# A two-layer block (window attention, then a scanned convolution): residuals laid into PSUM banks, row sums on ScalarE, accumulating DMAs, and the seven-product form from group 4 on

## The chip, the cores and the metric

The kernel runs on one core of a Trainium2 chip. The time is the device time of one execution in microseconds, lower is better. Before the change it is 2599.14 us, the median of 3 runs (2598.45 to 2602.19). All data is float32.

A core has a matrix engine (TensorE, PE in the profile; its weight loads are PEld), VectorE (DVE), ScalarE (ACT), GpSimd (POOL), and SyncE (SP), which here only issues DMAs. Each engine runs its own list of instructions in order, and waits for the others through semaphores. PSUM is the small memory that TensorE writes; it has banks, and a bank can be written again once its reader is done.

## The reference, cut to what matters

The input x has 2 images of 56 x 56 tokens with 384 channels. Two layers follow each other.

```
# layer 0
x = x + neighbourhood_attention(layer_norm(x)) @ w_proj + b_proj
x = x + gelu(layer_norm(x) @ w1 + b1) @ w2 + b2           # 384 -> 1536 -> 384
# layer 1
p      = layer_norm(x) @ w_in + b_in                      # 384 -> 768
local  = depthwise 3x3 convolution of p, padded
mixed  = 0.25 * (lr + rl + tb + bt) + local
x = x + layer_norm(mixed) @ w_out + b_out                 # 768 -> 384
x = x + gelu(layer_norm(x) @ w1 + b1) @ w2 + b2           # 384 -> 1536 -> 384
```

Each of `lr`, `rl`, `tb`, `bt` is a running average, y[i] = 0.6 y[i-1] + 0.4 local[i], along the rows forwards and backwards and along the columns forwards and backwards. The last step gives the output.

## The kernel before, in words

The attention takes the first 650 us or so and isn't touched. What follows works on token groups: 49 tiles of 128 tokens, a group being 4 tiles (512 tokens).

**The first pass** (13 groups: group 0 has one tile, groups 1 to 12 have four) computes the MLP of layer 0 and `p`. One step of the loop at L1712 does for its group g: 12 calls of `hidden` (L1191: 3 matmuls of 512 columns into a PSUM bank of which there are three, then a Gelu by ScalarE out of it), then `project_in` (L1471) for the group before, 6 times 3 matmuls with a ScalarE eviction each, stored to `p_d` in DRAM, then `tokens` (L1199) for 4 tiles, 12 matmuls of 384 columns each, in two banks by turns. VectorE takes each of these banks: it adds the residual `x` (L1846) and takes mean and variance of the sum (`Norm.add`, L214). In between, `ahead_of(m)` and `behind(m)` put a 1/12 of the work for the neighbouring groups after each hidden block: normalizing the previous group's result and the next group's input (ScalarE, L245), their statistics (VectorE), their transposes (TensorE) with the copy out of the bank (ScalarE, L262). Groups 1 and 2 compute the MLP by "seven products": a 2 x 2 block product done with seven block multiplications instead of eight (`hidden_by_seven`, L1536, `tokens_by_seven`, L1620), with the sums of blocks on GpSimd and VectorE. Group 3 is half of each form; from group 4 on the form is plain.

**The convolution** runs beside the matmuls from group 3 on, on VectorE. It works on 6 blocks of 128 channels. A `Band` (L1237) is a stretch of image lines of one block: it loads `p` from DRAM, ScalarE makes the centre tap (L1263), VectorE adds the eight other taps (L1281), stores `loc` to DRAM, scans the rows both ways (`both_ways`, L1225), adds `loc` (L1297) and stores the sum to `mix_d`. When all bands of an image are done, six `Columns` (L1306) follow: each loads `loc` of one block in two halves, turns it so that columns lie along the lines (four strided copies per half of the columns, by ScalarE, L1328; the first of a row of Columns by GpSimd), scans both ways in pieces of 14 lines (L1228, L1232), and adds the turned-back result to `mixed`, which was loaded from `mix_d` (L1355), then stores it.

**The second pass** (groups 0 to 12 again, the last of one tile) computes the rest: for each group `measure` (transposes of `mixed` by TensorE and their statistics by VectorE), `project_out` (L1434: `w_out`, 6 matmuls of 384 columns per tile, added to `x` by VectorE at L1440, with statistics), then `hidden`, `tokens` and the store. Up to group 5 the form is plain (loop L1885), from group 6 (`half_way`, the first group that reaches into image 1) it is by seven products (loop L1926). There VectorE also does the transposes, so that the convolution has to be over before: `beside.until` (L1390) puts all that is left of it into the program at that point, and the buffers of the seven-product form take the convolution's place.

**The planner** `Beside` (L115) sets the order. After each piece of the main work the program calls `beside.go(worth)`: it adds `rate * worth` to a budget, and steps of the convolution are written into the program until the budget is used up; each step says what it takes (`us(lines)`, L1221). `worth` is `MLP` = 2.25 per hidden block, `PRO` = 2.5 per block of `project_in`, `ROW` = 6.2 per tile of `tokens`, in the second pass 2.15, 2.5 and 7.0. So the planner decides, when the program is made, between which instructions of the main work each convolution instruction stands on every engine. `beside.later` issues a DMA one step later. Jobs are put on the list in `project_in` when enough groups of `p` exist (`BANDS`, L63): for image 0 after groups 2, 4, 5, 6, for image 1 after groups 8, 10 and 12.

## Time and profile before

| | |
|---|---|
| median of 3 runs | 2599.14 us |
| the profiled execution | 2598.4 us, its span 2596.6 us |
| PE busy | 2570.7 us, 99% |
| DVE busy | 1964.2 us, 76% |
| ACT busy | 982.9 us, 38% |
| POOL busy | 467.0 us, 18% |
| one plain group of the first pass, PE | 79.94 us |
| one plain group of the second pass, PE | 81.28 us |
| one group of the second pass by seven products, PE | 71.86 us |

The page gives busy time by engine, then the span in 40 slices (each digit is the busy share in tenths), then groups of instructions by line. In such a group stand the line, the engine, the operation, what it writes and reads, the count, then the busy time in us and the mean of one in ns, then the idle time ahead of it and what ended it. Instructions of one engine overlap a little, so that from one start to the next is shorter than "the mean of one": for ScalarE about 0.10 us shorter. One matmul in float32 stands as two records.

### The profile page before, as it was taken

The numbers are of one execution on the slowest core, as the hardware profiler recorded it, in microseconds if no ns is written. First come the engines' busy times: TensorE is split into PE (matmuls) and PEld (weight loads), VectorE is DVE, ScalarE is ACT, GpSimd is POOL, SyncE is SP. The second block draws the span as 40 slices with busy tenths as digits, with TensorE's granted clock in tenths as the row PEclk, the third lists the DMA queues.
The fourth block names the chain that finished last, engine by engine and source line by source line (L and its number), as shares of the span: only waits on it lengthen the run. The fifth ranks groups of instructions, "written<-read, shape, count | busy, mean of one in ns | idle before, by whom it ended". The sixth has DMA issues, their size and how long they took to land. (4 is left out here: it accounts for less than half of the span.)

```text
span 2596.6 us, 39994 instructions
## 1 busy us (share of the span) xinstructions
PE 2570.7 (99%) x16146; PEld 1644.1 (63%) x16148; DVE 1964.2 (76%) x3481; ACT 982.9 (38%) x1748; POOL 467.0 (18%) x457
## 2 busy tenths in 40 slices
PE   9999999999999999999999999999999999999999
PEld 5666666666798644555555555555555557888888
DVE  4888878887444288688998889889988836888871
ACT  5656555654443332322344423212233312333222
POOL 0111211121552100000010000000010042344432
PEclk9999999999999999999999999999999999999999
DMA  7423454225311132332346534533354321111000
GB/s 230 154 85 98 155 191 141 86 93 192 114 34 37 59 128 84 109 115 100 127 153 237 199 120 168 180 124 122 105 213 172 136 101 46 49 49 49 22 13 18
DMA packets 131652, 299.17 MB, mean 115 GB/s; under 512 B 10390, under 2 KB 85760, under 8 KB 129152
## 3 DMA queue, kind: packets, MB, share of 16 engines
q1 hardware_dynamic: 126512, 269.76, 30.2%
q10 hardware_dynamic: 4944, 26.74, 3.0%
q8 instruction: 129, 2.11, 0.3%
q14 instruction: 67, 0.55, 0.1%
HBM read 180.86 MB, written 115.61 MB: 114 GB/s over the span
## 5 line engine op out<-in xcount | busy, mean ns | idle before, releaser
L1185 PE MATMUL mm<-hT,w 128*128 128x512 f32 x1080 | 473.6, 593 | 0.1
L1281 DVE SCALAR_TENSOR_TENSOR loc<-pt,taps,loc 128x990 f32<-128x990 f32 (+9 forms) x336 | 377.2, 1123 | 10.2 <-ACT loc L1263 1.9
L1185 PEld LDWEIGHTS mm<-hT,w 128*128 128x128 f32 x1080 | 201.8, 190 | 239.0 <-issue 231.4
L227 POOL TENSOR_TENSOR rs<-rs,mhalf 128x4 f32<-128x4 f32 (+4 forms) x72 | 89.3, 1240 | 1269.9 <-DVE rs L224 1261.3
L1196 ACT ACTIVATE hid<-mm,chan 128x512 f32<-128x512 f32 x180 | 123.3, 686 | 405.9 <-PE mm L1185 405.8
L1203 PE MATMUL y<-w,hid 128*128 128x384 f32 x792 | 260.9, 486 | 0.0
L1203 PE MATMUL y_end<-w,hid 128*128 128x384 f32 x792 | 260.8, 486 | 0.0
L551 DVE TENSOR_TENSOR pts<-sc,bias 119x448 f32<-119x448 f32 (+5 forms) x396 | 219.3, 617 | 45.4 <-PE sc L540 45.1
L561 ACT ACTIVATE pts<-pts 119x448 f32<-119x448 f32 (+5 forms) x396 | 210.9, 573 | 112.1 <-DVE pts L551 107.2
L1203 PEld LDWEIGHTS y_end<-w,hid 128*128 128x128 f32 x792 | 149.9, 190 | 102.8
L1203 PEld LDWEIGHTS y<-w,hid 128*128 128x128 f32 x792 | 149.8, 190 | 102.8 <-issue 0.5
L394 PE MATMUL ps<-hT,wqkv 128*128 128x448 f32 x504 | 204.8, 550 | 2.1 <-ACT vs L439 1.5
L1185 PE MATMUL mm<-hT,w_in 128*128 128x512 f32 x396 | 172.0, 593 | 1.5 <-DVE hid_u L1571 0.9
L394 PEld LDWEIGHTS ps<-hT,wqkv 128*128 128x128 f32 x504 | 91.3, 189 | 84.4 <-issue 74.2
L1185 PEld LDWEIGHTS mm<-hT,w_in 128*128 128x128 f32 x396 | 75.0, 190 | 96.2 <-issue 91.9
L1168 DVE STREAM_TRANSPOSE hT<-xn 32x96 f32<-32x96 f32 x464 | 125.0, 269 | 11.6 <-ACT xn L245 5.6
L245 ACT ACTIVATE xn<-xc,sh,rs 128x384 f32<-128x384 f32 x98 | 64.4, 699 | 170.2 <-DVE sh L238 170.1
L1414 DVE STREAM_TRANSPOSE turned<-mx 32x192 f32<-32x192 f32 x336 | 124.0, 369 | 4.4
L580 PE MATMUL o<-pts,vt 100*32 100x112 f32 (+3 forms) x3168 | 117.0, 265 | 1.8 <-ACT pts L561 1.8
L540 PEld LDWEIGHTS sc<-qT,kT 32*100 32x100 f32 (+3 forms) x3168 | 87.8, 169 | 46.9 <-DVE sum L570 7.6
L540 PE MATMUL sc<-qT,kT 32*100 32x112 f32 (+3 forms) x3168 | 106.5, 268 | 3.5 <-DVE pts L551 3.5
L610 PE MATMUL ps<-wproj,og 128*128 128x384 f32 x294 | 106.4, 501 | 2.8 <-DVE og L523 2.1
(179 smaller groups left out, 4144.4 us busy)
## 6 DMA issues: line engine op xcount, KB each, us to landing
loc<-loc_d SPq DMA_DIRECT2D x24, 784.0 KB
mixed<-mix_d SPq DMA_DIRECT2D x24, 784.0 KB
mix_d<-mixed SPq DMA_DIRECT2D x24, 784.0 KB
xa<-x_d SPq DMA_DIRECT2D x24, 768.0 KB
bias<-in_bias_t ACTq DMA_DIRECT2D x13, 1344.0 KB
p_d<-mx SPq DMA_DIRECT2D x11, 1536.0 KB
mx<-mix_d SPq DMA_DIRECT2D x11, 1536.0 KB
pt<-p_d SPq DMA_DIRECT2D x18, 560.0 KB
```

Of the source, the lines that this page charges most:

```text
L394: nc.tensor.matmul(ps, lhsT=wqkv[:, c, m * P : (m + 1) * P], rhs=hT[:, c, half_of(n)], start=c == 0, stop=c == NC - 1,)
L540: nc.tensor.matmul(sc[i // 2][: w.keys, i % 2, q : q + TT], lhsT=kT[d, hg, w.keys_at + r * w.kc : w.keys_at + (r + w.rows) * w.kc], rhs=qT ...
L551: nc.vector.tensor_tensor(self.pts[:n, h : h + 2, lo:hi, :], sc[half][:n, :, at * TT : (at + hi - lo) * TT].rearrange("p h (c q) -> p h c ...
L561: nc.scalar.activation(t, t, AF.Exp)
L580: nc.tensor.matmul(o[i * HD : (i + 1) * HD, self.slot, :TT], lhsT=w.vt[:n, c, h * HD : (h + 1) * HD], rhs=self.pts[:n, i, c, :], start=c = ...
L610: nc.tensor.matmul(ps, lhsT=ogs[t // 7][:, c, at : at + P], rhs=wproj[:, c, :], start=c == 0, stop=c == NC - 1,)
L1168: nc.vector.transpose(hT[j : j + HD, :, k * P + i : k * P + i + HD], xn[i : i + HD, k, :].rearrange("p (c q) -> p c q", c=NC)[:, :, j : j ...
L1185: nc.tensor.matmul(ps[:, : n * P], lhsT=w[:, c, m * P : (m + 1) * P], rhs=hT[:, c, : n * P], start=c == 0, stop=c == NC - 1,)
L1196: nc.scalar.activation(t[:, : n * P], ps[:, : n * P], AF.Gelu, bias=col(b1, m))
L1203: nc.tensor.matmul(ps, lhsT=t[:, k * P : (k + 1) * P], rhs=w[:, m, :], start=m == 0, stop=m == len(lhs) - 1,)
L1281: nc.vector.scalar_tensor_tensor(to, pt[:, lo + dy - self.top : hi + dy - self.top, xt : xt + n], self.tap(dy, dx), to, ALU.mult, ALU.add,)
L1414: nc.vector.transpose(t[j : j + HD].rearrange("p (m c) -> p m c", m=NI)[:, :, i : i + HD], mx[i : i + HD, :, k * P + j : k * P + j + HD],)
```

## The change

- **Residuals laid into banks.** From group 3 of the first pass on, ScalarE copies the residual tile `x` into the PSUM bank (`seeded`), and the matmuls of `tokens` add onto it. VectorE's addition at L1846 goes.
- **Sums and statistics by ScalarE.** `ByScalar` takes the place of `Norm` for groups 3 and later, for the result and for the next group's input: `take` (ScalarE copy with a sum, and one GpSimd multiplication), `spread` (ScalarE Square with a sum) and `close` (four small GpSimd operations instead of one on VectorE and one on GpSimd).
- **Mixed channels by accumulating DMAs.** A Band stores `loc` into `mix_d` as well, ScalarE scales the scanned rows, and a DMA issued by GpSimd adds them to `mix_d` in DRAM. A Columns no longer loads `mixed`: ScalarE turns the scanned lines back, scaled (`turn_back`), and two DMAs add the halves to `mix_d`. VectorE's L1297 and L1355 go. Scans of Columns are one over 28 lines instead of two over 14.
- **Bias rows by accumulating DMAs.** `add_row` is a DMA issued by GpSimd instead of an addition on VectorE or GpSimd. `b_out` is added after `mix` has been loaded, in the second pass.
- **Seven products from group 4 on** in the second pass instead of from group 6 (`switch = 4`), with `beside.until` after `project_out` of group 4.
- **The planner's numbers:** `MLP`, `OUT`, `ROW` = 2.6, 3.9, 7.8, the rate 0.96 throughout, and in the second pass `STATS` = 0.75 is taken off the budget for each statistic that VectorE still does.

```diff
@@ class Beside
-        self.late, self.rate = [], 0.9
+        self.late, self.rate = [], 0.96
...
-    def later(self, issue):
+    def later(self, issue, steps=1):
-        self.late.append([1, issue])
+        self.late.append([steps, issue])
...
-    def go(self, worth):
-        self.due += self.rate * worth
+    def go(self, worth, own=0.0):
+        self.due += self.rate * worth - own
@@ class ByScalar (new)
+        def take(self, k, ps, out):
+            at = slice(k, k + 1)
+            nc.scalar.activation(out, ps, AF.Copy, accum_out=self.sum[:, at])
+            nc.gpsimd.tensor_tensor(self.off[:, at], self.sum[:, at], per_c[:, at], ALU.mult)
+        def spread(self, k, x, junk):
+            at = slice(k, k + 1)
+            nc.scalar.activation(
+                junk, x, AF.Square, bias=self.off[:, at], accum_out=self.var[:, at]
+            )
+        def close(self, k):
+            rs, tt = self.rs[:, :k], nc.gpsimd.tensor_tensor
+            tt(rs, self.var[:, :k], eps_c[:, :k], ALU.add)
+            tt(rs, rs, mhalf[:, :k], ALU.pow)
+            tt(rs, rs, root[:, :k], ALU.mult)
+            tt(self.sh[:, :k], self.off[:, :k], rs, ALU.mult)
@@ passes
-        half_way = next(g for g, (t, n) in enumerate(dgroups) if t + n * P > T1)
+        switch = 4
@@ def add_row
-            engine = nc.vector if beside.busy() else nc.gpsimd
-            engine.tensor_tensor(
-                x[:, :n, :], x[:, :n, :], row(name).unsqueeze(1).to_broadcast([P, n, C]), ALU.add
+            nc.gpsimd.dma_start(
+                out=x[:, :n, :], in_=row(name).unsqueeze(1).to_broadcast([P, n, C]),
+                accum_op=ALU.add,
             )
@@ new
+        def seeded(x, k):
+            ps = bank()
+            nc.scalar.copy(ps, x[:, k, :])
+            return ps
+        def primed(t):
+            nc.tensor.matmul(t, lhsT=zeros[:, :P], rhs=zeros[:, : t.shape[1]], start=True, stop=True)
@@ Band.steps
-                beside.later(lambda: nc.sync.dma_start(
-                    out=loc_d[self.b][self.m, :, at], in_=flat(loc)))
-                both = half("both", "out", 3)[:, : self.n]
...
-                nc.vector.scalar_tensor_tensor(
-                    flat(both), flat(both), share, flat(loc), ALU.mult, ALU.add
-                )
...
+                for to in (loc_d, mix_d):
+                    beside.later(lambda to=to: nc.sync.dma_start(
+                        out=to[self.b][self.m, :, at], in_=flat(loc)))
+                both = half("both", "out", 4)[:, : self.n]
+                yield from both_ways(both, loc)
+                behind = beside.behind()
                 if isinstance(behind, Band):
                     behind.centre()
+                beside.later(lambda: nc.scalar.mul(flat(both), flat(both), share), 5)
+                beside.later(lambda: add_to_mix(self.b, self.m, at, both), 8)
+        def add_to_mix(b, m, at, src):
+            nc.gpsimd.dma_start(out=mix_d[b][m, :, at], in_=flat(src), accum_op=ALU.add)
@@ Columns.steps
+                def turn_back(c):
+                    if not mixed:
+                        mixed.extend(half("mixed", "out", 4) for h in range(2))
                     for i in range(0, HALF, QUARTER):
                         at = slice(c * HALF + i, c * HALF + i + QUARTER)
                         for h in range(2):
-                            nc.vector.scalar_tensor_tensor(
-                                to, t[:, i : i + QUARTER, h * HALF : (h + 1) * HALF]
-                                .rearrange("p w h -> p h w"), share, to, ALU.mult, ALU.add,
+                            nc.scalar.mul(
+                                mixed[h][:, :, at],
+                                self.lines[c][:, i : i + QUARTER, h * HALF : (h + 1) * HALF]
+                                .rearrange("p w h -> p h w"), share,
                             )
+                for c in range(2):
+                    if c == 1:
+                        behind = beside.behind()
+                    for step, took in enumerate(both_ways(self.lines[c], self.lines[c])):
+                        if c == 0 and step == 0:
+                            self.turn(nc.scalar.copy)
+                        yield took
+                    beside.later(lambda c=c: turn_back(c), 1 + c)
                 if isinstance(behind, Columns):
                     behind.turn(nc.scalar.copy)
                 for h in range(2):
+                    beside.later(lambda h=h, at=at: add_to_mix(self.b, self.m, at, mixed[h]), 3)
@@
-        MLP, PRO, ROW = 2.25, 2.5, 6.2
-        MLP_D, OUT_D, ROW_D = 2.15, 2.5, 7.0
+        MLP, OUT, ROW = 2.6, 3.9, 7.8
+        STATS = 0.75
@@ first pass, groups 4 and later (before: statistics by VectorE at m == 3, normalizing from m == 7)
+                    if g >= EARLY.stop and 2 <= m < 2 + n_next:
+                        norm_next.take(m - 2, x_next[:, m - 2, :], xn_next[:, m - 2, :])
+                    if g >= EARLY.stop and 3 <= m < 3 + n_next:
+                        norm_next.spread(m - 3, x_next[:, m - 3, :], xn_next[:, m - 3, :])
+                    if g >= EARLY.stop and m == 2 + n_next:
+                        norm_next.close(n_next)
+                    if to <= m < to + n_next:
+                        norm_next.apply_by_scalar(m - to, x_next, xn_next)
...
+                    if g > EARLY.stop and m in (8, 10):
+                        seeds.append(seeded(x, m // 2 - 4))
...
-                ps = tokens(hid, w2, k)
-                nc.vector.tensor_tensor(x2[:, k, :], ps, x[:, k, :], ALU.add)
-                norm.add(k, [x2[:, k, :]])
+            for k in range(n) if g >= EARLY.stop else ():
+                norm.take(k, tokens(hid, w2, k, onto=seeds.pop(0)), x2[:, k, :])
+                if k + 2 < n:
+                    seeds.append(seeded(x, k + 2))
+                if k:
+                    norm.spread(k - 1, x2[:, k - 1, :], x[:, k - 1, :])
+                beside.go(ROW)
@@ second pass
-        for g, (t0, n) in enumerate(dgroups[:half_way]):
+        for g, (t0, n) in enumerate(dgroups[:switch]):
...
+            x3, norm = project_out(g + 1, *ahead)
+            ahead = load_mix(g + 2)
+            if g == switch - 1:
+                beside.until((1, NI - 1))
                 cctx.close()
                 tp = pctx.enter_context(tc.tile_pool(name="tail", bufs=1, reuse_waits="tile"))
                 three = wp.tile([P, NC, INNER], F32, name="w1_t", tag="w_in")
                 w1_sums = sums_of_w1(w1, three)
```

Besides, the normalizing of the previous group moves from m = 2 to m = 3, the line buffers become three deep and the output buffers four deep, the decay constants become 28 lines long and are written by GpSimd, and the descriptor space of GpSimd's DMAs is doubled.

## The prediction

> **What bounds the kernel now.** I read the page first, then the busy time in stretches, then the waits of TensorE and the lines of ScalarE.
>
> ```profile
> span 2596.6 us, 39994 instructions
> PE 2570.7 (99%) x16146; PEld 1644.1 (63%) x16148; DVE 1964.2 (76%) x3481; ACT 982.9 (38%) x1748; POOL 467.0 (18%) x457
> DVE  4888878887444288688998889889988836888871
> ACT  5656555654443332322344423212233312333222
> ```
>
> TensorE is busy all the time; VectorE at eight or nine tenths in slices 14 to 32 (convolution), ScalarE at two to four there. The time is then TensorE's work plus what it waits. The waits of TensorE between 1400 and 2130 us:
>
> ```profile
> PE y L1203 <- DVE xc L1440: 1.0, 1, 1.0
> PE mm L1185 <- ACT hT L262: 0.6, 1, 0.6
> ```
>
> So nearly nothing is waited for; only less work on TensorE shortens the kernel. The stretches are a first-pass group without Columns, one with them, a plain group of the second pass, one by seven products:
>
> ```profile
> 1232.19:1312.12 79.93, 79.93 (x229) 41.28 (x228) 73.27 (x108) 25.64 (x39) 3.26 (x2) 1.00 0.33 113
> 1392.06:1472.85 80.79, 80.20 (x230) 41.20 (x228) 67.78 (x81) 39.32 (x55) 3.81 (x2) 1.00 0.56 211
> 1993.51:2074.79 81.28, 81.28 (x253) 44.73 (x252) 68.97 (x85) 29.15 (x39) 3.36 (x2) 1.00 0.45 168
> 2183.18:2255.04 71.86, 71.54 (x349) 61.39 (x348) 60.37 (x167) 21.46 (x43) 29.53 (x26) 1.00 0.13 44
> ```
>
> (Columns: length, then PE, PEld, DVE, ACT, POOL, clock, DMA share, GB/s.) Two groups change from 81.28 to 71.86. The second row is longer than the first by 0.86 us, and ScalarE's list there says why:
>
> ```profile
> 1413.44 0.70 ACT L245 ACTIVATE xn<-xa,sh,rs 128x384 f32<-128x384 f32 x1
> 1414.04 3.40 ACT L1328 COPY line<-loc 128x392 f32<-128x392 f32 x4
> 1417.35 0.68 ACT L1196 ACTIVATE hid<-mm,chan 128x512 f32<-128x512 f32 x1
> ...
> 1419.69 3.43 ACT L1328 COPY line<-loc 128x392 f32<-128x392 f32 x4
> 1423.02 0.68 ACT L1196 ACTIVATE hid<-mm,chan 128x512 f32<-128x512 f32 x1
> 1423.61 0.70 ACT L245 ACTIVATE xn<-xa,sh,rs 128x384 f32<-128x384 f32 x1
> 1424.20 2.10 ACT L262 ACTIVATE hT<-tp,chan 128x512 f32<-128x512 f32 x3
> ```
>
> Two bursts of turned copies (3.3 us each from start to start) came before the copies of the transposes, and TensorE's `project_in` waits for those without slack. The work that the change takes off VectorE and puts on ScalarE is this kind:
>
> ```profile
> L1328 ACT COPY line<-loc 128x392 f32<-128x392 f32 x88 | 75.0, 928 | 69.9 <-DVE mixed L1355 53.5 <-DMA loc<-loc_d 16.3
> L1355 DVE SCALAR_TENSOR_TENSOR mixed<-line,mixed 128x392 f32<-128x392 f32 x96 | 77.9, 869 | 7.2 <-DMA mixed<-mix_d 7.2
> L227 POOL TENSOR_TENSOR rs<-rs,mhalf 128x4 f32<-128x4 f32 x24 | 42.2, 1758 | 913.6 <-DVE rs L224 913.6
> ```
>
> [...] L227 takes 1.76 us beside the convolution (row above, 950 to 1900 us), 1.01 for the same size in the seven-product groups.
>
> **The change part by part.**
>
> *Seven products from group 4.* 2 x (81.28 - 71.86) = 18.8 us less TensorE work. The 1.3 us that group 5 lost (82.58 against 81.28; the wait at L1440 behind GpSimd's sums for the switch) and the 0.86 us above go too, if nothing replaces them: 2.1 us. `primed` adds two matmuls like L1698's (0.39 us each): +0.8.
>
> *Does the convolution end in time?* Step costs in the code: a Band of 18 lines is 8 x 1.25 + 2.62 + 2.42 = 15.0 (real: 8 x 1.27 + 2 x 2.29, also about 15), a Columns 3.85 + 3.65 + 3.85 + 3.65 = 15.0. A first-pass group pays (18 x 2.6 + 4 x 7.8) x 0.96 = 74.9, a second-pass one (12 x 2.6 + 4 x 3.9 + 4 x 7.8) x 0.96 - 15 = 59.9. After the last release (group 12) there remain 6 x 16.5 + 6 x 15 + 10 for first loads = about 199; three groups pay 180, hidden and `project_out` of the fourth 33, together 213. It ends some 14 before `until`, in time. (The same count for the kernel before ends at the `until` itself, as its trace does: last L1355 at 2082 us.) VectorE itself has room: 735 us of convolution instead of 859 (L1297's 46 and L1355's 78 gone), and in the first pass nothing else, so its additions, statistics and rows are worth nothing to TensorE, which never waited for them.
>
> *ScalarE, ordinary group.* Per first-pass group, start to start: 12 Gelus and 6 evictions x 0.59, 8 normalizings x 0.60, 6 copies of transposes x 0.67 = 19.3. Added: four seeds x 0.38 (as L1659), `take` and `spread` twice four. [...] I take 0.6 to 0.7 and 0.8: 13 us. With five Bands (centre 1.1, scaling 0.9: 10 us) 42 of 80 us. Covered by three banks of slack.
>
> *ScalarE with Columns of image 0: the step that costs.* A Columns now has two turns and two turn-backs of four copies x 0.82 = 13.2 us of ScalarE in 15.0/0.96 = 16 us. Where they fall: bands of lines 47 to 56 are listed after `project_in` of group 6; by the budgets, `tokens` of group 7 and nearly all hidden blocks of group 8 (30 each) go into bands, so Columns 0 falls on `project_in`, 1 and 2 on `tokens` of group 8, 3 and 4 on the 12 hidden blocks of group 9, 5 on its `project_in`. By the delays in `later`, the order in the hidden blocks is: turn-back after m = 2 and 3, two turns after 5, turn-back after 8 and 9, two turns after 11; and turn-back and two turns (9.9 us) stand behind `take(3)`, which waits for the last `tokens`. I follow the queue from that point (0 = end of `tokens`): take 0.6, spread 0.8, 9.9, carried lateness 1.5, spread 0.8: ScalarE reaches the first Gelu at 13 instead of 2.6. Up to the copies of the transposes come 19.8 of turned copies, 11 Gelus 6.4, normalizings 4.2, `take` and `spread` of the next input 6.0, two seeds 0.8, the three copies 2.0: 39. So `project_in` starts at 52 instead of 32.2 (12 x 2.576 + 1.3): **+20 us**. The backlog left behind it (10 us) is worked off under `tokens`, which have 7.7 us of slack per tile. Queued behind the late ScalarE are TensorE, then everything by program order. `close` is four GpSimd operations with VectorE's 3.5 us scans in front of each (1 to 4 us each), and the normalizing waits for it: between 0 and 8 us more; I take 2. Sum +22, from 14 (cheap sums, no wait) to 30.
>
> *Second pass with Columns of image 1.* 15.0 of budget there last 20 us, ScalarE has 13.2 + 3.5: fits, but 9.9 us stand in one burst after m = 0 and 1 of the hidden blocks of groups 2 and 3; a third bank is wanted after 12.9 and comes at 14.9 and 14.3: +2 and +1.4. VectorE's scans are 3.5 us now instead of 1.8, and wait for ScalarE's turn, with the evictions of `project_out` (3.9 us of slack), the statistics of `xi` and the output rows behind them: 0 to 8, I take 3.
>
> *DMAs and GpSimd.* A Columns moves 0.8 MB four times plus the accumulate's reading, as before, in 16 instead of 28 us: 4.8 MB, 300 GB/s; the stretch from 1900 to 1950 us did 255 GB/s at a DMA share of 0.69, so it fits if adding costs a read and a write. Hidden; if not, rival 2. `add_row` by DMA: issued 20 us and more before its reader, nothing. The switch: GpSimd's nine sums (about 19 us, as L1520 and L1610) need the convolution's buffers free, and have 31 us of `tokens`: 0, I leave 1 with the other bank changes.
>
> Sum against the profiled execution's own 2598.4 (span 2596.6 and 1.8 around it): -18.8 - 2.1 + 0.8 + 22 + 3.4 + 3 = +8.3, so 2606.7; the median stands 0.7 above that execution: **2607**.
>
> **Rivals.**
> 1. *The gain stands* (faster). ScalarE is at 38% and a group with twelve turned copies in its hidden blocks lost only 0.86 us; if turn-backs are cheaper than turns or spread better, only -18.8 - 2.1 + 0.8 and some 3 in the second pass are left: 2581. Against it: 51 us of work in 32. Chance 0.20. It decides where the stall falls under 15 us.
> 2. *Accumulating DMAs bound the Columns.* If adding costs three passes, a Columns needs 6.4 MB at about 370 GB/s (255/0.69) = 17 us plus the groups' own 2: over 16; `turn_back` waits for its output buffer, ScalarE with it, Gelus behind. 1 to 5 us x 12, beside the main sum: 2620 to 2665. Or GpSimd[...] is late with `off`. Chance 0.15.
> 3. *The convolution is late at the new switch.* The margin is 14; ScalarE's lateness lengthens program and planner alike, but waits of VectorE for turns beyond 3 us per Columns use it up, and from there each us is one of TensorE's. 2605 to 2620. Chance 0.06.
> 4. The main case, mostly 2595 to 2617: 0.59.
>
> **How the numbers follow.** Within 0.2% (5 us) is what a measurement of this kernel can't tell from no change. Main case: 0.03 faster, 0.15 same, 0.41 slower; rival 1: 0.19 and 0.01; rival 2: 0.15 slower; rival 3: 0.01, 0.03, 0.02. Faster 0.23, same 0.19, slower 0.58. The range, 2582 to 2630, leaves out half of rival 1's low end and most of rival 2. Likeliest case alone: 2595 to 2617.
>
> **What would show it.** In the profile after: two more groups at 71.9 us; in one first-pass group (about 1305 to 1340 us) TensorE idle by some 20 us before `project_in`, ScalarE busy without a gap, its turned copies twice as many; no wait of TensorE for VectorE in the first pass; last scan before the `until`. I am wrong if that group takes 80 us as the others do, if ScalarE's turn-backs wait for DMAs, or if the next seven-product group starts late.

## The result, and the profile after

The changed kernel takes 2639.08 us (median of 4 runs, 2635.13 to 2641.22), the kernel before, run beside it, 2600.01 us: a ratio of 1.0148, 95% interval 1.0130 to 1.0165. It is slower by 39 us, where 8 were forecast, and lies above the range, which ended at 2630. The profiled execution takes 2637.5 us with a span of 2635.6, against a span of 2596.6 before.

The page of the kernel after, the lines that answer to those of before:

```profile
span 2635.6 us, 41141 instructions
PE 2566.0 (97%) x16318; PEld 1678.9 (64%) x16318; DVE 1842.4 (70%) x3421; ACT 1215.2 (46%) x2279; POOL 633.2 (24%) x719
DVE  3888878887343494889656938568774688788871
ACT  4665555654444354544776444322473323323222
```

VectorE lost 122 us of work and ScalarE gained 232. VectorE's digits fall to 6, 5 and 6 in slices 20 to 22, where ScalarE's are 7, 7 and 6: the Columns of image 0. In place of the two waits of TensorE shown before (1.6 us together) stand, between 850 and 2070 us:

```profile
PE mm L1226 <- ACT hid L1237: 30.4, 6, 10.4
PE mm L1226 <- ACT hT L303: 12.5, 3, 8.9
PE xi L1437 <- DVE st L227: 1.4, 1, 1.4
```

Both large ones are ScalarE: its Gelus (L1237) and its copies of the transposes (L303). The same four kinds of stretch as in the prediction (length, then busy time of PE, PEld, DVE, ACT, POOL, clock, DMA share, GB/s): a first-pass group without Columns, the one from 1285 us with Columns of image 0 (its `hidden` blocks begin at 1316 us; below it is "the group at 1316 us"), most of a second-pass group with Columns of image 1, and a group by seven products.

```profile
1105.21:1185.15 79.94, 79.94 (x229) 41.29 (x228) 72.86 (x69) 38.78 (x77) 17.14 (x23) 1.00 0.66 180
1285.25:1402.85 117.60, 89.63 (x231) 44.15 (x229) 74.00 (x33) 98.12 (x153) 40.72 (x28) 0.87 0.61 152
1965.00:2047.70 82.70, 77.07 (x228) 41.26 (x229) 38.19 (x41) 34.76 (x47) 29.37 (x19) 0.94 0.52 123
2081.30:2152.69 71.39, 71.39 (x349) 61.40 (x348) 57.22 (x167) 21.52 (x43) 25.40 (x26) 1.00 0.28 67
```

The first row has the length that it had (79.93). In the second, 117.60 instead of 79.94, ScalarE works 98.1 us and waits 19.4: for `close` 10.7, for an output buffer 5.5, for a load 2.6, and for TensorE only 0.6:

```profile
ACT xn L253 <- POOL norm_sh L284: 10.7, 2, 8.3
ACT mixed L1394 <- DMA mix_d<-both: 5.5, 1, 5.5
ACT xn L270 <- DMA xa<-x_d: 2.6, 1, 2.6
ACT mx L1508 <- PE mm L1226: 0.4, 1, 0.4
```

So here ScalarE's queue sets the length: its work is 18 us over the 80 of a group, and its waits add 19. Two numbers say that TensorE also runs slower: TensorE is "busy" for 89.63 us with the work of 79.94, and the clock is 0.87. The fourth row is what the change was made for, 71.39 instead of 81.28.

To count the loss I took each spacing from start to start of TensorE's instructions between 850 and 2070 us, less the median spacing of the same line and operands. An excess over 0.65 us is a wait; excesses of 0.25 to 0.65 us come in rows just after waits and are slow matmuls. Before: 3.0 us in all. After: 63.5, of which 37.0 in the group at 1316 us (28.8 waits + 8.2 slow), 19.6 in two second-pass groups (13.9 + 5.7), 5.5 elsewhere, the rest in shares too small for either. The sum closes: +60.5, less 2 x (81.28 - 71.40) = 19.8, less 4 x 0.46 because groups 6 to 9 take 71.40 now instead of 71.86, less the 1.3 of group 5, and 0.8 for the primed banks make +38.4; measured between the two profiled executions +39.0.

**What the slow matmuls are.** Windows of the kernel after on the matmuls that follow a wait of 4.3 us, and on those after them, columns as above:

```profile
1364.40:1367.70 3.30, 3.30 (x6) 1.24 (x5) 3.30 (x2) 0.00 (x0) 3.22 (x2) 0.50 0.42 175
1368.00:1370.40 2.40, 2.40 (x6) 0.92 (x6) 2.33 (x3) 0.00 (x0) 2.32 (x2) 0.98 0.00 0
```

The granted clock is 0.50, then 0.98: spacings of 0.43 us become 0.85, for three to nine of them after a wait, 1.4 to 3.0 us in all. In this kernel none of the five waits of 0.9 to 2.1 us was followed by slow matmuls, and each of the seven from 2.2 to 10.5 us was. In this kernel and five of those below together no wait of 2.14 us or less was followed by them, of 18 between 2.19 and 3.85 us ten were, and of those from 4.12 on all; what decides between the two lengths is not shown. The prediction did not price it. What it costs is another matter: where ScalarE is late anyway, as in the group at 1316 us, slow matmuls shorten the next wait of TensorE, and only the 2.65 us after its last wait have none behind them. The 8.2 us are part of the count, and not shown to be a cause of their own.

**ScalarE in the group that loses most.** A part of its list, to lay beside the one from 1413 us in the prediction (start, length, line, count, idle time ahead and what ended it):

```profile
1354.52 6.64 ACT L1375 COPY line<-loc 128x392 f32<-128x392 f32 x8
...
1362.82 1.27 ACT L1237 ACTIVATE hid<-mm,chan 128x512 f32<-128x512 f32 x2
1372.40 0.71 ACT L253 ACTIVATE xn<-xa,norm_sh,norm_rs 128x384 f32<-128x384 f32 x1 [8.31 <-POOL norm_sh L284]
1373.01 0.47 ACT L1254 COPY y<-xa 128x384 f32<-128x384 f32 x1
1373.42 0.91 ACT L1394 ACTIVATE mixed<-line 128x392 f32<-128x392 f32 x1
```

Eight turned copies in one burst of 6.6 us, and then 8.3 us in which ScalarE does nothing: it waits for the `close`. GpSimd's list says why:

```profile
1363.02 2.05 POOL L281 TENSOR_TENSOR norm_rs<-norm_var,eps_c 128x4 f32<-128x4 f32 x1 [8.71 <-ACT xn L275]
1365.14 4.08 POOL L282 TENSOR_TENSOR norm_rs<-norm_rs,mhalf 128x4 f32<-128x4 f32 x1
1369.30 2.79 POOL L283 TENSOR_TENSOR norm_rs<-norm_rs,root 128x4 f32<-128x4 f32 x1
1372.16 0.20 POOL L284 TENSOR_TENSOR norm_sh<-norm_off,norm_rs 128x4 f32<-128x4 f32 x1
```

The last runs free and takes 0.20 us; the power takes 1.0 us where it runs free (1000.71 us in the same trace). Beside VectorE's scans of 3.4 us, which stand at 1361.65, 1364.99 and 1368.67, they take 2.0 to 4.1: the addition and the multiplication end as a scan ends, the power 0.8 us after one. The prediction had 1 to 4 us for each operation and took 2 us for the whole wait, an estimate beside the power's 1.76 us in the kernel before (1.01 without the convolution); what in the two engines makes the operations late is not shown. The scans are 3.4 us long because the change makes one over 28 lines out of two over 14 (1.8 us before); no run undoes this.

The page's group of GpSimd's new multiplication in `take`, and ScalarE's groups that answer to L1355 and L1328, these between 850 and 2070 us:

```profile
L271 POOL TENSOR_TENSOR norm_off<-norm_sum,per_c 128x1 f32<-128x1 f32 x76 | 43.5, 572 | 462.0 <-ACT xc L270 384.1
```

```profile
L1394 ACT ACTIVATE mixed<-line 128x392 f32<-128x392 f32 x96 | 80.8, 918 | 15.0 <-DMA mix_d<-both 5.5 <-issue 4.8 <-DVE line L1283 4.7
L1375 ACT COPY line<-loc 128x392 f32<-128x392 f32 x88 | 73.8, 922 | 36.0 <-issue 18.4 <-DMA loc<-loc_d 17.5
```

The copies cost what was forecast (0.92 us each), and the 96 of L1394 are the added ones. New is a wait of 5.5 us for an output buffer that an accumulating DMA still reads. The waits for loads of `loc`, 17.5 us, are hardly longer than before (16.3), but now ScalarE has no time to spare for them.

### The profile page after: what moved, and what is told of

Read it like the earlier page. It is cut to its first block, busy times and chain, and to the rows that moved or that the text cites. A ratio compares the mean times of both kernels' runs of the same rounds, so it can differ in the third digit from the quotient of the medians.

```text
span 2635.6 us, 41141 instructions
## 1 busy us (share of the span) xinstructions
PE 2566.0 (97%) x16318; PEld 1678.9 (64%) x16318; DVE 1842.4 (70%) x3421; ACT 1215.2 (46%) x2279; POOL 633.2 (24%) x719
## 5 line engine op out<-in xcount | busy, mean ns | idle before, releaser
L1226 PE MATMUL mm<-hT,w 128*128 128x512 f32 x936 | 423.5, 607 | 32.6 <-ACT hid L1237 30.4
L1226 PEld LDWEIGHTS mm<-hT,w 128*128 128x128 f32 x936 | 178.8, 195 | 249.9 <-issue 201.6
L1209 DVE STREAM_TRANSPOSE hT<-xn 32x96 f32<-32x96 f32 x720 | 194.1, 270 | 84.2 <-PE mm L1226 59.4
L1244 PE MATMUL y<-w,hid 128*128 128x384 f32 x696 | 229.3, 486 | 0.0
L1244 PE MATMUL y_end<-w,hid 128*128 128x384 f32 x696 | 229.2, 486 | 0.0
L1226 PE MATMUL mm<-hT,w_in 128*128 128x512 f32 x396 | 174.9, 600 | 11.9 <-ACT hT L303 10.4
L1449 DVE STREAM_TRANSPOSE turned<-mx 32x192 f32<-32x192 f32 x464 | 171.2, 369 | 6.1
L1237 ACT ACTIVATE hid<-mm,chan 128x512 f32<-128x512 f32 x156 | 105.2, 681 | 126.1 <-PE mm L1226 125.9
L271 POOL TENSOR_TENSOR norm_off<-norm_sum,per_c 128x1 f32<-128x1 f32 x76 | 43.5, 572 | 462.0 <-ACT xc L270 384.1
L235 POOL TENSOR_TENSOR rs<-rs,mhalf 128x4 f32<-128x4 f32 (+4 forms) x55 | 58.0, 1054 | 336.4 <-DVE rs L232 326.5
L1279 DVE TENSOR_TENSOR_SCAN line<-decay,line 128x1568 f32<-128x1568 f32 x24 | 81.8, 3410 | 75.2 <-ACT line L1375 60.9
L547 POOL COPY totals<-turned 128x12 f32<-128x12 f32 x56 | 20.2, 360 | 387.8 <-DVE turned L542 377.6
```

Source lines behind the costliest of these rows:

```text
L1209: nc.vector.transpose(hT[j : j + HD, :, k * P + i : k * P + i + HD], xn[i : i + HD, k, :].rearrange("p (c q) -> p c q", c=NC)[:, :, j : j ...
L1226: nc.tensor.matmul(ps[:, : n * P], lhsT=w[:, c, m * P : (m + 1) * P], rhs=hT[:, c, : n * P], start=c == 0, stop=c == NC - 1,)
L1237: nc.scalar.activation(t[:, : n * P], ps[:, : n * P], AF.Gelu, bias=col(b1, m))
L1244: nc.tensor.matmul(ps, lhsT=t[:, k * P : (k + 1) * P], rhs=w[:, m, :], start=m == 0 and onto is None, stop=m == len(lhs) - 1, skip_group_c ...
L1279: nc.vector.tensor_tensor_scan(flat(dst), d, flat(src), 0.0, ALU.mult, ALU.add)
L1449: nc.vector.transpose(t[j : j + HD].rearrange("p (m c) -> p m c", m=NI)[:, :, i : i + HD], mx[i : i + HD, :, k * P + j : k * P + j + HD],)
```

## The experiments

Theory A: the loss is ScalarE in the Columns, by its load and by the waits that stand inside its queue. Theory B: it is the accumulating DMAs, and the transfers that they delay. Theory C: it is the sums and statistics that ScalarE does in the first pass. The table gives for each kernel the median, the ratio to the kernel before, and TensorE's lost time as counted above, waits + slow matmuls, by place. Both sides count: a run whose total falls can hide one place behind another. The kernels were measured in four lots, and the kernel before took 2600 us beside the first five changed kernels of the table, 2596 to 2597 beside the next six, 2598 beside the last two; so totals of different lots are compared by their ratios (0.0010 is 2.6 us). The lost time is that of one execution, and leaves out the first 850 us, in which these executions also differ: they come to the first `project_in` after 857 to 865 us.

| kernel | us | ratio (95%) | group at 1316 us | second pass | elsewhere |
|---|---|---|---|---|---|
| before | 2600.0 | 1 | 0 | 0 | 1.8 + 0.3 |
| after | 2639.1 | 1.0148 (1.0130-1.0165) | 28.8 + 8.2 | 13.9 + 5.7 | 5.2 + 0.3 |
| copies back by VectorE | 2624.7 | 1.0089 (1.0066-1.0112) | 22.9 + 6.7 | 8.7 + 3.7 | 9.2 + 3.3 |
| close by VectorE | 2636.4 | 1.0139 (1.0119-1.0159) | 20.6 + 6.1 | 14.9 + 6.2 | 13.6 + 1.9 |
| plain stores | 2633.6 | 1.0132 (1.0113-1.0151) | 29.9 + 8.0 | 11.0 + 4.9 | 4.2 + 0.3 |
| statistics by VectorE | 2646.7 | 1.0181 (1.0164-1.0198) | 8.9 + 1.6 | 14.0 + 7.1 | 29.4 + 6.8 |
| both: copies and close | 2630.5 | 1.0135 (1.0119-1.0152) | 11.4 + 4.6 | 8.4 + 3.7 | 16.5 + 7.2 |
| turn one step later | 2617.9 | 1.0083 (1.0066-1.0100) | 21.6 + 6.8 | 9.6 + 2.3 | 4.2 + 0.3 |
| switch at 6 | 2660.6 | 1.0255 (1.0235-1.0275) | 30.0 + 7.8 | 14.2 + 5.8 | 4.2 + 0.6 |
| spread out | 2601.6 | 1.0021 (1.0013-1.0029) | 8.3 + 1.7 | 6.5 + 0 | 5.2 + 1.9 |
| ... sums earlier | 2605.5 | 1.0034 (1.0018-1.0050) | 10.3 + 3.1 | 4.7 + 1.6 | 6.1 + 2.3 |
| ... close by place | 2603.0 | 1.0028 (1.0018-1.0038) | 11.6 + 1.8 | 4.6 + 2.5 | 2.1 + 1.1 |
| ... load moved up | 2596.2 | 0.9995 (0.9987-1.0003) | 9.4 + 1.4 | 4.8 + 2.1 | 2.1 + 1.2 |
| ... rate 0.97 | 2593.8 | 0.9984 (0.9976-0.9991) | 5.0 + 2.7 | 5.9 + 3.0 | 1.6 + 0.3 |

### The copies back on VectorE

```diff
-                            nc.scalar.mul(
+                            nc.vector.tensor_scalar_mul(
                                 mixed[h][:, :, at],
```

> The turned-back copies of the Columns go to VectorE (tensor_scalar_mul, same shapes, no step cost added, so the program order of everything else stays). Theory A (ScalarE's Columns work and the waits inside it are the loss): 96 copies of 0.82 us leave ScalarE; the first-pass group that loses 38 us at 1316 to 1384 us loses at most 10, the two second-pass groups that lose 20 lose about 10, and the time falls from 2639 to 2595 to 2612. Theory B (the accumulating DMAs and the transfers they delay are the loss): the same DMAs run, so the time stays over 2625. Theory C (the sums and statistics on ScalarE are the loss): the time falls by no more than 10.

It gave 14 us, half of what A had: 2624.7. A's range is missed, and in the group at 1316 us, where A had at most 10 us, 29.6 are lost. B wanted more than 2625, which a miss by 0.3 us neither bears out nor refutes, and C's bound of 10 us is passed. The trace tells where A's gain went. ScalarE's largest wait and the group of VectorE's copies in this run, between 1300 and 1385 us:

```profile
ACT xn L253 <- POOL norm_sh L284: 19.5, 2, 11.4
```

```profile
L1394 DVE TENSOR_SCALAR mixed<-line 128x392 f32<-128x392 f32 x32 | 14.3, 509 | 0.0
```

With a third of its work in this group gone (64.6 us instead of 98.1), ScalarE waits 19.5 us for the two closes instead of 10.7: the load was hiding them. Another 11.3 us of waits are new, for VectorE's copies, which hold the line buffers. ScalarE now has less work than the 80 us of a group, and still TensorE loses 29.6 us: the waits in the queue count, not only its load. And the same strided copy that costs ScalarE 0.82 us from start to start costs VectorE 0.43.

### The close on VectorE

```diff
-            rs, tt = self.rs[:, :k], nc.gpsimd.tensor_tensor
+            rs, tt = self.rs[:, :k], nc.vector.tensor_tensor
             tt(rs, self.var[:, :k], eps_c[:, :k], ALU.add)
-            tt(rs, rs, mhalf[:, :k], ALU.pow)
+            nc.gpsimd.tensor_tensor(rs, rs, mhalf[:, :k], ALU.pow)
```

> Three of the four small operations of the first pass's close (add, root, shift) go from GpSimd to VectorE, the power stays on GpSimd. Theory A with its waits: in the group at 1316 us ScalarE stood idle 2.4 and 8.3 us for a close whose four GpSimd operations took 2.0 to 4.1 us each beside VectorE's scans; with one left the two waits fall to 3 us or less together, and the time falls by 6 to 10, to about 2631. If the wait only covers other work that is late anyway (pure load), the time stays within 3 us of 2639.

In its place the expectation held: the two waits fell from 10.7 to 0.6 us, and TensorE's loss in the group from 37.0 to 26.7. But elsewhere it rose from 5.5 to 15.5, since a close on VectorE stands behind that engine's taps in the groups with Bands: between 900 and 1300 us ScalarE waits 11.0 us for it instead of 4.0. The range for the time is missed: the total, 2636.4, says nearly nothing, and by the total alone the wait would have been called harmless.

### Plain stores

```diff
-            nc.gpsimd.dma_start(out=mix_d[b][m, :, at], in_=flat(src), accum_op=ALU.add)
+            nc.gpsimd.dma_start(out=mix_d[b][m, :, at], in_=flat(src))
```

> The 24 stores of the Columns and those of the Bands into mix_d are plain writes on the same GpSimd queue instead of accumulating ones; this leaves the local term out of the mix. Theory A: only the 5.5 us that ScalarE waits at 1303 us for an output buffer and some of the 13 us that it waits for loads in the second pass can shrink: 2630 to 2639. Theory B: at least 15 us go, below 2624.

2633.6: the adding costs 5 us at most, and theory B's number is missed. (This run keeps the number of stores and their place in GpSimd's queue; what those cost isn't tested.) The accumulating ones are dear in themselves (784 KB take 9.7 us from issue to landing, the plain ones 4.9), but TensorE's loss at 1316 us is the same (37.9 for 37.0), and ScalarE still waits 5.9 us for the output buffer there. That buffer was the last of A's claims: it is late because its DMA stands in GpSimd's queue behind a multiplication by `off` that takes 3.3 us beside a scan, and the DMA (252 KB) lands 4 to 5 us after its issue with adding (4.2 in the kernel after) and without. The 3.7 us of the second pass go with loads of `loc` that arrive earlier (10.1 us of waiting instead of 13.4).

### The additions and statistics of the first pass back on VectorE

```diff
-                norm.take(k, tokens(hid, w2, k, onto=seeds.pop(0)), x2[:, k, :])
...
+                ps = tokens(hid, w2, k)
+                nc.vector.tensor_tensor(x2[:, k, :], ps, x[:, k, :], ALU.add)
+                norm.add(k, [x2[:, k, :]])
```

> First pass as in the kernel before in its additions and statistics (VectorE adds the residual and does the statistics; no seeds, no sums on ScalarE), all else as in the kernel after, step costs too. Theory A: in the group at 1316 us ScalarE loses about 10 us of work and the close becomes one GpSimd operation, so its loss falls from 38 to about 18 and the 20 us of the second pass stay: 2615 to 2625. Theory C: nearly all of the loss goes, below 2605. If VectorE is too full for the additions, evictions come late and the time rises above 2639.

Slower, 2646.7, by neither A's nor C's number. Its local claim holds and more: the group at 1316 us loses 10.5 us instead of 37.0. The row of this group, to lay beside the 117.60 above:

```profile
1302.08:1393.11 91.03, 82.96 (x230) 41.46 (x229) 78.91 (x55) 85.97 (x114) 19.08 (x14) 0.98 0.79 195
```

It has 80 turned copies in it, against 82 in the kernel after. But without the sums and seeds ScalarE works 86.0 us instead of 98.1, and it waits 1.2 us for statistics instead of 10.7 for `close`. So in this place the sums and the close are as much of the cause as the copies. But elsewhere VectorE falls behind: it has additions and statistics again that the planner's numbers don't allow for, and ScalarE's queue now holds the scaling of each Band's scanned rows. ScalarE's waits of this kind between 900 and 1500 us:

```profile
ACT both L1347 <- DVE both L1283: 168.7, 19, 22.1
ACT xn L253 <- DVE sh L246: 40.3, 11, 9.9
```

The first is 8.3 us in the kernel after. Of the 29.4 us of TensorE's waits elsewhere, 9.4 stand behind the scaling (L1347), alone or with the normalizing; 6.7 behind the normalizing alone, which waits for VectorE's statistics; 8.3 are waits for VectorE itself, and 5.1 come behind a late load. How much of this other planner's numbers would have spared isn't tested. Theory C is wrong for the whole, since the second pass keeps its loss (21.1 us), and holds for a good part in the group at 1316 us.

### The two edits together

> The two edits together: turned-back copies and three of the four operations of the close on VectorE, the power on GpSimd. In the kernel with the copies moved alone ScalarE still stood 8.1 and 11.4 us for the two closes, and in the one with the close moved alone it had no such wait but 13 us more copies. Theory A (load and close waits are two limits in parallel, each hiding the other's removal): together they give more than the sum of 14 and 3: the group at 1316 us loses under 10 us instead of 38, and the time is 2600 to 2612. If the two merely add: 2620 to 2624.

In the group they do work together (37.0 to 16.0; alone 29.6 and 26.7), but the time is 2630.5: the loss elsewhere is 23.7 us, from closes that wait behind taps and, at 1415 us, a seed that TensorE waited 4.1 us for, because ScalarE stood 16.3 us before a Band's centre tap whose load was late. So the expectation failed for the whole, and in the group it had named under 10 us. By the trace the run loses 2 us less than the one with the copies alone; by the ratios, whose intervals stand apart, it takes 12 us more. The traced executions are the fastest of this run's and the slowest of the other's; what the rest is stays open.

### The turn one step later

```diff
-                        if c == 0 and step == 0:
+                        if c == 0 and step == 1:
                             self.turn(nc.scalar.copy)
```

> The kernel after with one edit: the turn of a Columns' second half is issued one step later, so that the bursts of four copies stand apart; the same copies, on ScalarE. Bursts as the cause of the second pass's 20 us: that part falls to about 10, the group at 1316 us stays near 38 (its load is unchanged): 2626 to 2632. Loads that arrive late as its cause (ScalarE waited 13.4 us for loc in the second pass): no change, 2636 to 2642. VectorE then waits up to 3 us per Columns for the turn, which can make it late: above 2642.

One digit gives 17 us by the ratios (the medians, of two lots, differ by 21), about as much as moving half of ScalarE's copies, and more than the 7 to 13 that were expected: 2617.9. No copy is saved. In the kernel after the first turn of a Columns, which the Columns ahead of it issues, and the turn of its second half stand next to each other in ScalarE's queue, the burst of eight seen above; now, in the second pass's hidden blocks, two Gelus stand between the fours. In the second pass 7.7 us go, though ScalarE waits as long for loads there as before (14.8 us for 13.4), so late loads alone were not the cause; at 1316 us 8.6 go as well, which had been put down to sheer load. (By the count of the trace it is 17 in all.) In this group ScalarE's work is the same (99.3 us for 98.1) and its waits fall from 19.4 to 9.7, those for `close` from 10.7 to 4.3. So the gain there came by shorter waits in ScalarE's queue; how much the distance of the bursts does by itself isn't separated. What remains of TensorE's waits between 1300 and 1400 us:

```profile
PE mm L1226 <- ACT hid L1237: 11.7, 4, 5.7
PE mm L1226 <- ACT hT L303: 9.1, 1, 9.1
```

How a burst and a late load combine is seen in the kernel after, in ScalarE's list of the second pass:

```profile
1973.28 0.69 ACT L1237 ACTIVATE hid<-mm,chan 128x512 f32<-128x512 f32 x1
1974.06 0.93 ACT L1375 COPY line<-loc 128x392 f32<-128x392 f32 x1
1979.55 5.79 ACT L1375 COPY line<-loc 128x392 f32<-128x392 f32 x7 [4.56 <-DMA loc<-loc_d]
1985.25 1.82 ACT L1237 ACTIVATE hid<-mm,chan 128x512 f32<-128x512 f32 x3
```

Within the burst the second half's load is late by 4.6 us, so that the Gelus are 12.0 us apart, where three banks cover 3 x 2.58.

### Seven products from group 6 again

```diff
-        switch = 4
+        switch = 6
```

> Seven products from group 6 on as before, all else as in the kernel after. Theory A: two groups of 71.4 become plain ones of 81.3, nothing else moves: 2639 + 19 = 2658 (2653 to 2663). If the earlier switch had itself cost something (a stall at the switch, a convolution that is hurried), the difference is smaller: 2640 to 2650.

2660.6, and 18.6 us between the two spans: the gain of the switch is there in full, and by the table the convolution pays nothing for the earlier end. By the ratios the difference is 28 us; the 9 beyond the traces' stay open.

### Spread out, and four runs further

```diff
                     for step, took in enumerate(both_ways(self.lines[c], self.lines[c])):
-                        if c == 0 and step == 0:
+                        if c == 0 and step == 1:
                             self.turn(nc.scalar.copy)
                         yield took
-                    beside.later(lambda c=c: turn_back(c), 1 + c)
+                    turn_back(c)
+                    yield 1.8
```

The turned-back copies and the close are VectorE's, as above, and the rate is 1.0. So this run and those after it show what can be reached, not what each edit gives.

> The two edits together, and besides: the turn of the second half is issued one step later, so that two bursts of four copies (3.3 us each) no longer stand side by side in ScalarE's queue; the copies on VectorE are charged at 1.8 us for four, and the rate is 1.0 instead of 0.96 so that the convolution ends as early. Theory A with bursts: the second-pass groups lose under 6 us instead of 20, the group at 1316 us under 6: 2588 to 2600, at or below the kernel before. If bursts don't matter: as the run before this one.

2601.6 (beside 2596.3 for the kernel before), where at most 2600 was expected: 10.0 us are lost at 1316 us and 6.5 in the second pass, where under 6 each had been named, and 7.1 elsewhere. No wait of TensorE for ScalarE is left in the second pass. The next runs went after the rest. First the load of the next input, for which ScalarE still waited 7.3 us:

```diff
-                    norm.spread(k - 1, x2[:, k - 1, :], x[:, k - 1, :])
+                    norm.spread(k - 1, x2[:, k - 1, :], junk[:, k - 1, :])
...
-                    if g >= EARLY.stop and 2 <= m < 2 + n_next:
-                        norm_next.take(m - 2, x_next[:, m - 2, :], xn_next[:, m - 2, :])
+                    if g >= EARLY.stop and 1 <= m < 1 + n_next:
+                        norm_next.take(m - 1, x_next[:, m - 1, :], xn_next[:, m - 1, :])
```

> The spread-out kernel (2601.6) with two more edits in the first pass: the squares that nobody reads go into the normalized tile that the transposes have left instead of into the group's input, so that the next input's load needn't wait for the last of them (ScalarE waited 7.3 us for that load at 1329 us); and the sums, squares and close of the next input come one hidden block earlier. Theory A: of the 25 us that TensorE still loses there, the 7 us of waits and slow matmuls around 1331 and some of the 3 us at 1264 go: 2589 to 2597, below the kernel before. If the copies of the group still fill ScalarE anyway: within 3 us of 2601.

A miss, 2605.5: the load is written into the program where it was, after `tokens`, so freeing its buffer earlier moved nothing, and a sum that is asked for one block sooner only waits longer for it (9.5 us). Next, `close` on GpSimd beside Bands and on VectorE beside Columns:

```diff
+            tt = nc.vector.tensor_tensor if on_columns else nc.gpsimd.tensor_tensor
```

> As the run before this one, but the close's three small operations are on VectorE only where Columns run and on GpSimd beside Bands, where the 18 closes on VectorE cost it 21.5 us of waiting for GpSimd's power. If these waits on VectorE reach TensorE (the wait at 1264 us): 2 to 5 us less than the run before this one. If VectorE has room: the same within 2 us.

By the trace 5 us elsewhere are saved (8.4 to 3.2 with the slow matmuls); by the time 2603.0, whose interval overlaps that of the run before. Then the load itself, at the third tile of `tokens` instead of after the fourth, with the sums where they were:

```diff
+                if k == 2 and g + 2 <= last:
+                    xs[g + 2] = load_group(x1f, groups[g + 2], "xa")
```

> The spread-out kernel with the close by place and the squares' output in the spent normalized tile as in the run before, sums and squares back at their hidden blocks, and the load of the input after next issued two tiles earlier in tokens (about 15 us), which the moved output allows. ScalarE waited 8.9 us for this load in the group at 1332 us. Theory A: that wait goes and with it most of the 9.6 us that TensorE waits for Gelus there and some 4 us of slow matmuls: 2589 to 2597. If the load is held by other loads ahead of it in SP's queue: within 3 us of 2603.

ScalarE no longer waits for that load, and waits 6.7 us for the close instead; TensorE's loss at 1316 us goes from 13.4 to 10.8 only, the expectation's "most" did not come. The time, 2596.2, fell by more than these 2.6 us (the ratio by 0.0033); the traces don't show the rest: both profiled executions have a span of 2599.0, the later one with 2.5 us more before its first `project_in`. Last, the rate:

> As the run before this one at a rate of 0.97 instead of 1.0: VectorE is given 3% less convolution per TensorE time; the convolution still ends before the switch. If the 3.8 us that TensorE waits for the statistics of xi in the second pass come from a VectorE that is behind: 2 to 5 us less than the run before. If the position of the Columns in the groups matters more than the rate, either sign, within 8 us.

2593.8, the lowest time: 0.9984 of the kernel before, interval 0.9976 to 0.9991, and by the ratios 43 us below the kernel after. From the run before it is not told apart, as the intervals overlap. The wait for the statistics of `xi` stayed, against the reason given for it; the count of the trace falls at 1316 us. Its waits of TensorE from 850 to 2070 us:

```profile
PE xi L1448 <- DVE st L227: 5.6, 4, 4.2
PE mm L1230 <- ACT hid L1241: 4.2, 1, 4.2
PE y L1248 <- DVE xc L1489: 1.4, 1, 1.4
```

19.8 us are lost in all, still as much as two groups by seven products gain. So it ends near the kernel before.

## Why the prediction was right or wrong, point by point

- **Seven products, -18.8: right.** 71.39 us per group instead of 81.28, and 18.6 us by the traces when undone. That a bit more came (groups 6 to 9 take 0.46 less) was not foreseen.
- **Small stalls, -2.1: wrong in part.** The one of group 5 went; the 0.86 us before a `project_in` came back as 1.7 and 1.0 in two other groups, and 1.6 and 0.9 us appeared before the first transposes of `xi`. Together 5.2 us of waits where 1.8 stood.
- **Convolution in time: right.** The last scan starts at 1997.8 us, `tokens` after the `until` at 2023.2; 14 us had been worked out, some 22 are there.
- **First pass with Columns: the place and the kind right, the size wrong, 37 instead of 22.** The step that failed is the sum for ScalarE: it added up ScalarE's work and put its waits at 2 us. The work was sized about right (98.1 us in a group of 80: 18 too much, where 20 were taken), though its 0.6 to 0.7 us for `take` and 0.8 for `spread` were the author's estimate, which no trace of before showed: they take 0.46 to 0.52 and 0.60 from start to start. The waits inside its queue were 19.4 us. `close`: "between 0 and 8 us more; I take 2"; ScalarE waited 10.7, and the run with the close on VectorE lost 10.3 us less in this group. The output buffer (5.5) and the load of the next input (2.6) had no term. Nor had slow matmuls, 8.2 us of the count. That order matters, and not only the sum, the turn one step later shows: with the same work ScalarE waits 9.7 us less. `project_in` starts 67.2 us after the end of `tokens`, where 52 were forecast; but only 9.1 of the 28.8 us of waits stand right before it, the others between the hidden blocks. "ScalarE busy without a gap" was wrong, and the sign "if ScalarE's turn-backs wait for DMAs" came true with the 5.5 us.
- **Second pass, 2 + 1.4 + 3: wrong, 19.6.** The bursts were seen and priced at 2 and 1.4; they cost 5.9 and 5.8 us of waiting, since in each a load of `loc` was late (0.9 and 4.6 us) and behind the first stood the scaling of a Band. That bursts are part of the cause, the turn one step later shows (11.9 us lost instead of 19.6); 2.2 came where copies of transposes were late behind a burst, and 5.7 in slow matmuls. VectorE's scans, for which 3 us were set aside, cost nothing there.
- **DMAs and GpSimd hidden: wrong.** The adding itself costs 5 us at most. But GpSimd's part is seen in ScalarE's waits (10.7 and 5.5 us above), and loads of `loc` come late in the second pass, 13.4 us of ScalarE's time. The bias rows by DMA were not undone in any run; no wait of TensorE names them.
- **Rival 1** (the gain stands) is out: the stall it wanted under 15 us is 37. **Rival 2** named the right range for the time and the wrong reason: the run with plain stores stays at 2634. Its last clause, GpSimd late with `off`, is the one that was true, once, where an `off` of 3.3 us beside a scan held back the DMA of an output buffer; GpSimd was late above all with the `close`. **Rival 3** is out.

So by the count of TensorE the 32 us between forecast and time are 14 of slow matmuls, 7 of waits in the group at 1316 us beyond the 22, 7.5 of waits in the second pass beyond the 6.4, and some 4 of small stalls elsewhere. In the group at 1316 us the cause, seen from ScalarE, is its waits. A term of 1 us, left "with the other bank changes", is missing from the prediction's sum, which changes nothing.

## What to carry to other kernels

When an in-order engine takes on new work, write out its queue in the tightest stretch with every wait in it, not only the sum of its work: here 98 us of work came with 19 us of waits, and eight copies side by side cost more than the same copies with Gelus in between. After a wait of over 4 us on TensorE count the slow matmuls too (here at a granted clock of 0.50, 1.4 to 3 us in all), unless TensorE is soon to wait for the same late engine again. And when an experiment removes one of several overlapping waits, read the place in the trace, since the total can stay while the cause is gone.

## What the runs showed of the hardware

- GpSimd's operations on 4 elements a partition (kernel after): 0.20 us alone and 1.0 for the power; beside VectorE's 3.4 us scans 2.0 to 4.1 us, the four of a `close` in a row for 9.3 and 10.5 us.
- A strided copy with a factor, 392 elements: 0.82 us from start to start on ScalarE (kernel after), 0.43 on VectorE (copies back by VectorE).
- An accumulating DMA of 784 KB into DRAM: 9.7 us from issue to landing (kernel after), 4.9 without adding (plain stores).
- ScalarE's sum output is read in an instruction of its own, 0.19 us as recorded, 0.09 from start to start (kernel after).
- TensorE's matmuls at twice their spacing (0.85 us for 0.43, granted clock 0.50 in the kernel after) for three to nine of them after every wait over 4.1 us in six of these kernels, after ten of 18 between 2.19 and 3.85, and after none under 2.19.
